# Splitting the small tables one pass per step over the first two tiles, and evicting the counts by plain copies

## Chip, cores, metric

One core of one Trainium2 chip. The metric is the device time of one execution in microseconds (us), the median of several. Most executions agree within 0.3%. Every run quoted here is in the state called fast. A ratio of two kernels is the mean time of one kernel's fast runs over that of the other's in the same rounds on the same chip, so it isn't quite the ratio of the medians that are quoted. The experiments fell on three different chips; on two of them the kernel before takes 7170 us in place of 5298, which is told with the experiments.

## The reference

A recommender network for 16384 rows: 32 word embeddings of 300 numbers and 3 x 20 embeddings of 64 from small tables are averaged, four more rows are looked up singly, and the 748 features go through dense layers of 1024, 512, 256 and 1, to which a sum of one-column tables is added.

```python
tok = word_emb[token_idx].mean(axis=1)          # 50000 x 300, 32 per row
e1 = emb_mh1[mh1_idx].mean(axis=1)              # 1000 x 64, 20 per row; mh2 (5000), mh3 (10000) alike
o1 = emb_oh1[oh1_idx]                           # 100, 50, 20, 1000 rows, one per row
emb = jnp.concatenate([tok, e1, e2, e3, o1, o2, o3, o4], axis=1)
wide = wide_mh1[mh1_idx].sum(axis=(1, 2)) + ...
h = relu(emb @ W1 + b1); h = relu(h @ W2 + b2); h = relu(h @ W3 + b3)
return sigmoid(h @ Wd + bd + wide)
```

## The kernel before

The work runs in 128 tiles of 128 rows. Word rows are gathered from HBM by indirect DMAs that POOL (GpSimd) issues, 32 per tile (128 rows of 300 each), and DVE (VectorE) adds them up, with the sum in PSUM. Buffers hold 6 groups of two gathers. The small tables (138 slices of 128 rows, 65 columns with the wide one) stay in SBUF, the memory on the chip. For them DVE makes one-hot matrices, TensorE (PE) multiplies them to counts, ACT (ScalarE) evicts the counts from PSUM to fp8, and PE multiplies counts by tables. So that bf16 tables are exact enough, each table is split into three bf16 terms: ACT rounds, DVE subtracts what was rounded off, twice. A tile has 11 steps, and all engines go through their instructions in program order.

```python
def convert_tables():                       # PART = 46 slices, CHUNK = 23
    raws = [load_tables(k * PART, tags[k]) for k in range(2)]
    yield
    for part in range(n_h // PART):
        raw = raws[part]
        for a in range(0, PART, CHUNK):
            rows = raw[:, a : a + CHUNK, :]
            for c in range(3):
                at = part * PART + a
                term = terms[:, at : at + CHUNK, c * ROW : (c + 1) * ROW]
                scale = 2.0 if c == 0 else 1.0
                nc.scalar.activation(term, rows, AF.Copy, scale=scale)
                if c < 2:
                    nc.vector.scalar_tensor_tensor(
                        rows, rows, scale, term, op0=ALU.mult, op1=ALU.subtract)
            yield
        ...

def counts(cnt, hot, i):
    pc = ps_c.tile([P, 2, 2, 512], F32, name="pc")           # one PSUM buffer
    ...                                                      # 12 matmuls
    nc.scalar.activation(cnt[...], pc[...], AF.Copy, scale=0.5, saturate=True)

# a step i of tile t (cut)
hot = one_hots(sc, s, i + 1)                                 # DVE
counts(cnt, hot_now, i)                                      # PE, ACT
if t == 0 and i % 3:
    next(tables_on_chip, None)                               # one whole chunk
toks.to(n_groups * (i + 1) / STEPS)                          # gathers (POOL), additions (DVE)
...                                                          # products with the tables, dense layers
```

## Time and profile before

Three runs: 5286.8, 5298.4 and 5295.36 us, median 5295.36. The profiled execution spans 5284.0.

| stretch of the gathers | us | what sets it |
|---|---|---|
| tile 0 | 75.4 | POOL waits for DVE, which works in turn with ACT on the tables |
| tiles 1 to 125 | 40.0 each | 32 gathers of 0.95 us and 0.30 between them |
| from tile 126 to the end | 201 | TensorE, as far as the trace tells: the dense layers of the last tiles (POOL waits here, and PE is busy 36 to 41 us of every 39 to 42) |

In the group lines the columns are: busy time, mean ns of one instruction, then the idle time ahead of them and what ended most of it. In the timelines: start, length, engine, source line, operation, and in brackets how long the engine had been idle and what released it. The lines themselves stand in the prediction.

### The profile page before, as it was taken

Reading aid. Unit: us, or ns where it says so; the run is one execution under the profiler, and the core shown is the slowest. Engines: PE = TensorE matmul, PEld = TensorE weight load, DVE = VectorE, ACT = ScalarE, POOL = GpSimd, SP = SyncE. Lnnn points to the kernel's source line nnn. Section 1 sums busy time; section 2 is a strip of 40 time slices with the busy share of each in tenths; the row PEclk is TensorE's granted clock in tenths of the full one; section 3 lists DMA queues with packets and bytes.
Section 4 is the critical chain, followed back from the end, with each engine's and each line's share of the span. In section 5 each row is a group of like instructions: output and inputs, shape, how many; then the busy total and the mean of one; then the engine's idle time right before and its main releaser. Section 6 shows DMA issues by size and latency. Waiting matters only on the chain.

```text
span 5284.0 us, 104301 instructions
## 1 busy us (share of the span) xinstructions
PE 5073.1 (96%) x41320; PEld 3160.4 (60%) x41320; DVE 3763.4 (71%) x8014; ACT 2528.4 (48%) x2000; POOL 3881.2 (73%) x4103
## 2 busy tenths in 40 slices
PE   3699999999999999999999999999999999999999
PEld 3556565666565666666566556556656556655658
DVE  6777777777777777777777777777777777777753
ACT  5444444444444444444444445445444444444433
POOL 5777777777777777777777777777777777777762
PEclk9799999999999999999999999999999999999999
DMA  6444444444444444444444444444444444444431
GB/s 167 125 124 126 126 126 126 126 125 125 126 126 126 126 124 126 126 125 126 125 125 125 126 126 125 124 125 126 125 126 125 124 126 125 126 126 125 124 103 34
DMA packets 245354, 652.60 MB, mean 124 GB/s; under 512 B 108977, under 2 KB 111988, under 8 KB 244863
## 3 DMA queue, kind: packets, MB, share of 16 engines
q0 software_dynamic: 196608, 629.41, 43.4%
q1 hardware_dynamic: 48255, 16.53, 1.4%
q8 instruction: 323, 5.29, 0.4%
q14 instruction: 168, 1.38, 0.1%
HBM read 645.59 MB, written 0.07 MB: 122 GB/s over the span
## 4 chain that ended last, share of the span: by engine, by line
PE 26%; DMA 26%; issue 17%; DVE 17%; POOL 12%; ACT 1%; SPq 0%; DVEq 0%; POOLq 0%; ACTq 0%
DMA tok_rows<-in_word_emb_dram,it 25%; PE ph L387 14%; POOL tok_rows L223 12%; PE pg L336 8%; DVE own L214 5%; DVE own L212 3%; PE pc L311 3%; DVE slice L293 3%; DVE row L293 1%; DVE x L378 1%; DVE g L342 1%; DVE own L210 1%; PE po L412 1%; DMA raw<-in_mh_dram 0%; ACT cnt L318 0%
## 5 line engine op out<-in xcount | busy, mean ns | idle before, releaser
L223 POOL DMA_INDIRECT tok_rows<-in_word_emb_dram,it x4096 | 3880.3, 947 | 1324.0 <-issue 754.2
L318 ACT ACTIVATE cnt<-pc 128x1656 fp8e3<-128x1656 f32 (+1 forms) x1408 | 2120.6, 1506 | 2020.2 <-PE pc L311 2004.1
L336 PE MATMUL pg<-terms,cnt 128*128 128x195 bf16 x17664 | 1847.6, 254 | 83.1 <-DVE g L342 81.4
L336 PEld LDWEIGHTS <-cnt 128*128 128x128 fp8e3 x17664 | 1599.5, 144 | 229.1 <-issue 74.9
L387 PE MATMUL ph<-x,w_sb 128*128 128x512 f32 (+5 forms) x3264 | 1458.3, 576 | 0.5 <-DVE x L378 0.5
L214 DVE TENSOR_TENSOR own<-own,tok_rows 128x300 f32<-128x300 f32 x1792 | 857.1, 478 | 715.5 <-DMA tok_rows<-in_word_emb_dram,it 684.8
L387 PE MATMUL ph<-h,w_sb 128*128 128x512 f32 (+2 forms) x2720 | 1211.0, 573 | 0.0
L212 DVE TENSOR_TENSOR own<-own,tok_rows 128x300 f32<-128x300 f32 x1920 | 918.5, 478 | 400.3 <-DMA tok_rows<-in_word_emb_dram,it 348.6
L311 PEld LDWEIGHTS <-row 64*128 64x128 bf16 x16384 | 504.5, 95 | 1083.3 <-DVE own L214 255.7
L293 DVE TENSOR_TENSOR row<-own,sc 128x768 bf16<-128x768 bf16 (+1 forms) x1408 | 761.3, 541 | 156.5 <-PE pc L311 81.7
L311 PE MATMUL pc<-slice,row 64*128 64x138 bf16 x16384 | 759.1, 224 | 115.0 <-ACT cnt L318 72.2
L387 PEld LDWEIGHTS ph<-x,w_sb 128*128 128x128 f32 (+1 forms) x3264 | 560.3, 193 | 397.8 <-issue 394.0
L293 DVE TENSOR_TENSOR slice<-own,sc 128x828 bf16<-128x828 bf16 (+1 forms) x1408 | 796.2, 565 | 0.0
L387 PEld LDWEIGHTS ph<-h,w_sb 128*128 128x128 f32 x2720 | 463.1, 192 | 318.4 <-issue 316.3
L396 ACT ACTIVATE h<-ph,b_sb 128x512 f32<-128x512 f32 (+2 forms) x476 | 315.3, 662 | 684.8 <-PE ph L387 673.1
L342 DVE TENSOR_REDUCE g<-pg 128x130 f32<-128x390 f32 (+1 forms) x512 | 258.1, 504 | 108.7 <-PE pg L336 108.3
L378 DVE TENSOR_SCALAR x<-pt,scale 128x512 f32<-128x512 f32 (+4 forms) x204 | 137.2, 713 | 5.3 <-PE pt L377 3.4
L377 PE MATMUL pt<-ident,g 128*128 128x128 f32 (+1 forms) x768 | 103.2, 275 | 2.8 <-DVE x L378 2.3
L210 DVE TENSOR_TENSOR own<-tok_rows 128x300 f32<-128x300 f32 x128 | 61.5, 480 | 47.5 <-DMA tok_rows<-in_word_emb_dram,it 44.6
L377 PEld LDWEIGHTS pt<-ident,g 128*128 128x128 f32 (+1 forms) x768 | 85.5, 140 | 6.4 <-DVE x L378 5.4
L214 DVE TENSOR_TENSOR g<-own,tok_rows 128x300 f32<-128x300 f32 x128 | 60.2, 470 | 25.9 <-DMA tok_rows<-in_word_emb_dram,it 21.1
L412 PE MATMUL po<-h,wd_sb 128*1 128x512 f32 (+2 forms) x136 | 60.9, 566 | 0.3
(34 smaller groups left out, 369.1 us busy)
## 6 DMA issues: line engine op xcount, KB each, us to landing
tok_rows<-in_word_emb_dram,it POOLq DMA_INDIRECT x4096
ix<-in_idx_dram SPq DMA_DIRECT2D x128, 32.0 KB
w_sb<-in_W_dram SPq DMA_DIRECT2D x6, 512.0 KB
it<-in_idx_dram SPq DMA_DIRECT2D x32, 64.0 KB
w_sb<-in_W_dram SPq DMA_DIRECT2D x1, 2048.0 KB
raw<-in_mh_dram SPq DMA_DIRECT2D x1, 975.0 KB
out_dram<-h SPq DMA_DIRECT2D x31, 2.0 KB
raw<-in_mh_dram SPq DMA_DIRECT2D x1, 292.5 KB
```

Of the source, the lines that this page charges most:

```text
L212: nc.vector.tensor_add(tok_sum, tok_sum, a)
L214: nc.vector.tensor_add(to, tok_sum, b)
L223: nc.gpsimd.indirect_dma_start(out=rows[:, r * TOK_D : (r + 1) * TOK_D], out_offset=None, in_=word, in_offset=bass.IndirectOffsetOnAxis(ap ...
L293: nc.vector.tensor_tensor(one[:, 0:rows, :].rearrange("p i (n d) -> p i n d", d=2), iota[:, 0:n].rearrange("p (n d) -> p n d", d=2).unsque ...
L311: nc.tensor.matmul(pc[:, f, k // n, at : at + n_h], hot[0][half, k, :], hot[1][half, k, :], start=True, stop=True,)
L318: nc.scalar.activation(cnt[:, :, b : b + rows, :].rearrange("l f (g k) h -> l f g (k h)", g=2), pc[:, :, :, 0 : n * n_h], AF.Copy, scale=0 ...
L336: nc.tensor.matmul(pg[:, j, :], by_slice[:, :, h], terms[:, h, :], start=(h == h0), stop=(h == h1 - 1))
L342: nc.vector.tensor_reduce(g[:, at : at + n * ROW].rearrange("p (f d) -> p f d", f=n), pg[:, 0:n, :].rearrange("p f (c d) -> p f d c", c=3) ...
L377: nc.tensor.transpose(pt[:kk, s * P : (s + 1) * P], chunk(g, k), ident)
L378: nc.vector.tensor_scalar(x[:kk, k, 0:n], pt[:kk, 0:n], scale[:kk, k : k + 1], None, ALU.mult)
L387: nc.tensor.matmul(ph[:, 0:n], weights[:kk, k, m * P : (m + 1) * P], src[:kk, k, 0:n], start=(k == 0), stop=(k == len(kks) - 1),)
L396: nc.scalar.activation(dst[:, m, 0:n], ph[:, 0:n], AF.Relu, bias=bias[:, m : m + 1])
```

## The change

It intends to keep the first tile from standing still while the tables are split, and to take the clamp out of the count eviction, which a count of at most 20, halved, doesn't need (the results stay correct). A generator now yields after each of 18 passes in place of 6 chunks of five passes, and hands out 1.2 passes per step from step 3 on, so that the last is done in step 17 (step 6 of the second tile), just ahead of the products that need it. DVE's pass needs an ACT pass that is usually a step old. Loads go in parts of 23 slices, and the dense weights are loaded at the end of tile 1.

```diff
-    PART, CHUNK = n_h // 3, n_h // 6
+    PART = n_h // 6
...
         for part in range(n_h // PART):
+            rows = raws[part]
+            if 1 <= part < n_h // PART - 1:
+                raws.append(load_tables((part + 1) * PART, tags[(part + 1) % 2]))
+            for c in range(3):
+                term = [terms[..., k * ROW : (k + 1) * ROW] for k in range(3)]
+                if c:
+                    nc.vector.scalar_tensor_tensor(
+                        rows, rows, 2.0 if c == 1 else 1.0, term[c - 1], op0=ALU.mult, op1=ALU.subtract)
+                nc.scalar.activation(term[c], rows, AF.Copy, scale=2.0 if c == 0 else 1.0)
+                yield 1
...
-            saturate=True,
+            saturate=False,
...
-                if t == 0 and i % 3:
-                    next(tables_on_chip, None)
-                if t == 0 and i == STEPS - 1:
+                tables_on_chip.to(TABLE_PACE * (t * STEPS + i - 2))      # TABLE_PACE = 1.2
+                if t == 1 and i == STEPS - 1:
                     load_weights()
```

More of the change, by code (lines that the diff above doesn't have):

```diff
@@ L30 @@
 CHUNK_WORK = 1
+TABLE_PACE = 1.2
 LAYER_TIME = 10
@@ L165, in convert_tables @@
         for part in range(n_h // PART):
-            raw = raws[part]
-            for a in range(0, PART, CHUNK):
-                rows = raw[:, a : a + CHUNK, :]
-                for c in range(3):
-                    at = part * PART + a
-                    term = terms[:, at : at + CHUNK, c * ROW : (c + 1) * ROW]
-                    scale = 2.0 if c == 0 else 1.0
-                    nc.scalar.activation(term, rows, AF.Copy, scale=scale)
-                    if c < 2:
-                        nc.vector.scalar_tensor_tensor(
-                            rows, rows, scale, term, op0=ALU.mult, op1=ALU.subtract
-                        )
-                yield
-            if part + 2 < n_h // PART:
-                raws.append(load_tables((part + 2) * PART, tags[part % 2]))
+            rows = raws[part]
+            if 1 <= part < n_h // PART - 1:
+                raws.append(load_tables((part + 1) * PART, tags[(part + 1) % 2]))
+            for c in range(3):
+                term = [
+                    terms[:, part * PART : (part + 1) * PART, k * ROW : (k + 1) * ROW]
+                    for k in range(3)
+                ]
+                if c:
+                    nc.vector.scalar_tensor_tensor(
+                        rows, rows, 2.0 if c == 1 else 1.0, term[c - 1], op0=ALU.mult, op1=ALU.subtract
+                    )
+                nc.scalar.activation(term[c], rows, AF.Copy, scale=2.0 if c == 0 else 1.0)
+                yield 1
     w1_sb = const.tile([P, NK, D1], F32, name="w1_sb")
@@ L470 @@
     next(tables_on_chip)
+    tables_on_chip = Paced(tables_on_chip)
     sc = key_columns(lookup_keys(ix))
@@ L516 @@
         before = cnt if t < tiles else None
-        if t == 0:
-            for _ in tables_on_chip:
-                pass
         if len(gs) == sizes[0]:
```

## The prediction

> **What bounds the kernel now.** I read the page first, then the POOL timeline, then the order of work in the first tile, then a table of stretches. The work runs in 128 tiles of 128 rows; each tile gathers 32 token columns, one indirect DMA each, issued by POOL.
>
> ```profile
> PE 5073.1 (96%) x41320; PEld 3160.4 (60%) x41320; DVE 3763.4 (71%) x8014; ACT 2528.4 (48%) x2000; POOL 3881.2 (73%) x4103
> PE   3699999999999999999999999999999999999999
> POOL 5777777777777777777777777777777777777762
> L223 POOL DMA_INDIRECT tok_rows<-in_word_emb_dram,it x4096 | 3880.3, 947 | 1324.0 <-issue 754.2
> ```
>
> PE at 96% looks like the bound. The last line says otherwise: 4096 gathers of 947 ns, with 1324.0 us of idle time ahead of them, which is 0.32 us each, put down to "issue". So POOL does one gather after another, and 4096 x (0.947 + 0.30) is already 5108 us of the 5284. The POOL timeline shows that beat, and where it is lost:
>
> ```profile
> 15.78 0.95 POOL L223 DMA_INDIRECT tok_rows<-in_word_emb_dram,it  x1 [0.30 <-issue]
> 17.03 0.95 POOL L223 DMA_INDIRECT tok_rows<-in_word_emb_dram,it  x1 [0.30 <-issue]
> 33.24 0.95 POOL L223 DMA_INDIRECT tok_rows<-in_word_emb_dram,it  x1 [15.27 <-DVE own L210]
> ...
> 38.24 0.95 POOL L223 DMA_INDIRECT tok_rows<-in_word_emb_dram,it  x1 [0.30 <-issue]
> 39.49 2.46 POOL L223 DMA_INDIRECT tok_rows<-in_word_emb_dram,it  x1 [0.30 <-issue]
> 45.55 0.94 POOL L223 DMA_INDIRECT tok_rows<-in_word_emb_dram,it  x1 [3.60 <-DVE own L214]
> ...
> 75.94 0.95 POOL L223 DMA_INDIRECT tok_rows<-in_word_emb_dram,it  x1 [7.10 <-DVE own L214]
> ```
>
> Starts are 1.25 us apart, so a tile costs 32 x 1.25 = 40.0 us of issuing. The first tile's 32 gathers start at 3.07, and the first gather of the second tile starts at 78.44: 75.4 us, 35.4 us over the beat, in waits for DVE to add up rows and free a buffer. Taking every 32nd gather's start from the trace, each of the tiles 1 to 125 takes 40.0 us (the longest 40.3), and only the last two take 60.2, because their share of the dense layers is larger. So: first tile 75.4, then 125 tiles on POOL's beat, then from 5083 to 5284 a stretch in which PE is truly the bound. Why DVE is late in the first tile:
>
> ```profile
> 16.83 1.47 ACT L173 ACTIVATE terms<-raw 128x1495 bf16<-128x1495 f32 x1 [2.20 <-DMA raw<-in_mh_dram]
> 18.33 1.72 DVE L175 SCALAR_TENSOR_TENSOR raw<-raw,terms 128x1495 f32<-128x1495 f32 x1 [6.71 <-ACT terms L173]
> 20.08 1.47 ACT L173 ACTIVATE terms<-raw 128x1495 bf16<-128x1495 f32 x1 [1.78 <-DVE raw L175]
> 21.58 1.72 DVE L175 SCALAR_TENSOR_TENSOR raw<-raw,terms 128x1495 f32<-128x1495 f32 x1 [1.53 <-ACT terms L173]
> ...
> 24.70 1.52 ACT L318 ACTIVATE cnt<-pc 128x1656 fp8e3<-128x1656 f32 x1
> ```
>
> One piece of table (23 slices of 65) is split into three bf16 terms by ACT and DVE in turn: three ACT passes of 1.47 and two DVE passes of 1.72, each waiting for the other, about 8 us in which neither does anything else. The count eviction, ready since about 15.6, waits until 24.70. Six pieces do this in the first tile. The other matter is ACT's tables:
>
> ```profile
> 554.32 1.28 ACT L420 ACT_TABLE_LOAD   x1
> 556.29 0.68 ACT L420 ACTIVATE h<-po,bd_sb 1x512 f32<-1x512 f32 x1 [0.69 <-PE po L416]
> 556.99 1.28 ACT L318 ACT_TABLE_LOAD   x1
> 558.28 1.55 ACT L318 ACTIVATE cnt<-pc 128x1656 fp8e3<-128x1656 f32 x1
> ```
>
> Each sigmoid costs a load before it and one before the next count eviction. Two stretches, the first without such a pair and the second with it (columns: length, PE, PEld, DVE, ACT, POOL busy and their counts, clock, DMA share, GB/s):
>
> ```profile
> 480.00:520.00 40.00, 39.80 (x319) 24.06 (x318) 27.43 (x59) 18.60 (x15) 30.26 (x32) 1.00 0.45 124
> 520.00:560.00 40.00, 38.85 (x314) 23.45 (x314) 27.57 (x60) 21.78 (x18) 30.26 (x32) 1.00 0.46 125
> ```
>
> ACT is 3.2 us busier in the second and PE is 1 us less busy, but POOL issues 32 gathers in both.
>
> **What the Trainium skill says.** "ScalarE: Activation LUTs", section "What ACT_TABLE_LOAD costs": about 1283 ns for any set, and a drain on top; the trace has the same 1.28 us. The same page, section "Step-by-step: what each stage is for", gives one element per cycle and lane whatever the function, so a plain copy should be no faster than the clamping function; the trace of before has only the clamped form (1548 ns for 1656 elements) and a plain copy from SBUF (1466 ns for 1495), about the same per element. "FP8 and Floating Point Precision", section "Saturation and Rounding": the plain conversion does not saturate; a count beyond the range would matter to values, not to time. "SBUF — State Buffer", section "Who interferes with whom": a DVE instruction with two SBUF inputs contends with a GpSimd instruction that reads SBUF, and the second blocks. The trace agrees: the gather at 39.49 lasted 2.46 us instead of 0.95 beside the DVE pass from 39.42 to 41.14 (both inputs in SBUF), and two more, at 49.31 and 61.09, lasted 1.92 and 1.96.
>
> **The change part by part.**
> 1. Table loads. In the built programs ACT has 64 table loads before and 2 after: the clamped copy is a function of a set that has no sigmoid, the plain copy is in sigmoid's set. That removes 62 x 1.283 = 79.5 us of ACT busy time. I expect none of it on the path: POOL keeps its beat across the loads, and in the PE-bound end only the two pairs at 5158 and 5161 and the load at 5221 are left, where PE has other matmuls. Worth 0, at most 2 us.
> 2. Eviction itself: 1408 x the same duration. Worth 0.
> 3. Staggering. The same 18 ACT passes and 12 DVE passes remain, but one pass per step over steps 3 to 17 (11 steps a tile) instead of three per step in seven steps. In the new order a DVE pass needs an ACT pass of an earlier step, except in the steps with two passes (step 3, step 8, step 13). An ideal beat would bring the first tile from 75.4 to 40.0: worth 35.4.
> 4. What is given back. (a) The lock: a gather starts every 1.25 us, so each DVE pass of 1.72 meets at least one; from the three seen the extra is 1.5, 1.0, 1.0, and for a random phase about 1.6 - 0.63 = 1.0 us. 12 x 1.0 = 12 us. (b) DVE itself: a step needs two one-hots (0.54 + 0.57) and some 1.45 row-pair additions (2 x 0.48 each), 2.5 us; 15 steps with 12 passes are 37.5 + 20.6 = 58.1 us, plus about 2 us of waiting in each of the three double steps, 64 us, against 15 x 3.64 = 54.6 of the beat. POOL starts these steps some 4 us ahead in buffers. So DVE holds POOL back by 5 to 6 us. (a) and (b) overlap, since a POOL that waits for a buffer isn't hurt by the lock: I take 12 us together, over the first two tiles.
> 5. Weights are loaded a tile later (5.3 MB around 80 us instead of 42). First used in tile 5, at about 200 us: worth 0. Table loads of 23 slices: in the chain of waits, 46 slices took 11.9 us from 34.17, so 23 take about 6 to 7; they have two to three steps, 7 to 11 us, from buffer free to use: 0 to 2 us, inside the 12.
>
> Sum: 35.4 - 12 = 23 us, so 5295 - 23 = 5272; I say 5271, because two of the three runs before lie near the top of their spread (5286.8 to 5298.4). The profiled span should go from 5284 to about 5261.
>
> **The rivals.** (A) PE or ACT is the bound in the steady state, so that 31 pairs of loads are each worth 2.6 us: 80 us, and with the start 103, giving 5192, just at 2%. For it: PE at 39.8 of 40.0 us. Against it: 125 tiles of exactly 40.0 us, with and without loads, with and without dense layers. (B) The conversion is hidden completely: 5260. The lock speaks against it, seen three times. (C) Splitting is merely moved: the loads of parts 2 to 5 come late, or the queue order of ACT passes before the next count eviction makes two tiles of 52 us each: saving 11, 5284. For it: ACT is in order and counts have one PSUM buffer. Against: ACT needs only 1.55 + 1.47 = 3.0 of 3.64 us a step. (D) The first product of tile 1 with a table part that isn't ready would stall PE; by the order, part k is complete at steps 4, 7, 9, 12, 14, 17 and first used one to seven steps later, and PE has 27 of 40 us of work in tile 1: no loss.
>
> **Range and chances.** The saving lies between 11 (C) and 35 (B), with 23 likeliest; the median of three runs moves by about 5 by itself. 8 in 10: 5258 to 5285. Faster by over 2% needs more than 106 us, which only A nearly gives: 0.01. Slower by over 2%: 0.01. Within: 0.98.
>
> **What would show it.** Right: ACT busy falls by about 80 to some 2450; first gathers of tiles 1 and 2 start near 50 and 95 (78.44 and 118.47 before); gathers of 1.5 to 2.5 us beside DVE passes, a dozen of them; all later tiles 40.0 us; the stretch from tile 126 on still 201 us. Wrong: a tile below 40.0 us in the middle (POOL wasn't the beat), or tiles 0 and 1 at 40 (no lock), or waits of ACT for table data in tile 1.

## The result, and the profile after

The changed kernel took 5272.2 us (four runs, 5271.1 to 5273.52), the kernel before 5295.3 (four runs). The ratio is 0.9959, with an interval of 0.9942 to 0.9976: 0.4% faster, which counts as the same at a margin of 2%. The result is correct.

From the page of the changed kernel, the busy times and the gathers' group:

```profile
PE 5094.7 (97%) x41320; PEld 3164.7 (60%) x41320; DVE 3768.8 (72%) x8014; ACT 2447.1 (46%) x1938; POOL 3897.3 (74%) x4103
L224 POOL DMA_INDIRECT tok_rows<-in_word_emb_dram,it x4096 | 3896.4, 951 | 1293.4 <-issue 755.5
```

ACT has 62 instructions and 81 us less: the table loads. POOL's gathers were idle 31 us less ahead of them (1293.4 for 1324.0), and busy 16 us more (3896.4 for 3880.3). The idle time that went is the first tile's. Part of the busy time that came is seen in the first two tiles, in this timeline of the changed kernel (some lines of other work left out):

```profile
19.53 1.46 ACT L180 ACTIVATE terms<-raw 128x1495 bf16<-128x1495 f32 x1
...
21.03 1.72 DVE L177 SCALAR_TENSOR_TENSOR raw<-raw,terms 128x1495 f32<-128x1495 f32 x1 [4.22 <-ACT terms L180]
22.07 1.50 POOL L224 DMA_INDIRECT tok_rows<-in_word_emb_dram,it  x1 [0.30 <-issue]
22.78 1.47 ACT L180 ACTIVATE terms<-raw 128x1495 bf16<-128x1495 f32 x1 [1.78 <-DVE raw L177]
...
24.15 1.53 ACT L319 ACTIVATE cnt<-pc 128x1656 fp8e3<-128x1656 f32 x1
...
24.72 1.71 DVE L177 SCALAR_TENSOR_TENSOR raw<-raw,terms 128x1495 f32<-128x1495 f32 x1
25.16 2.09 POOL L224 DMA_INDIRECT tok_rows<-in_word_emb_dram,it  x1 [0.30 <-issue]
...
46.49 0.95 POOL L224 DMA_INDIRECT tok_rows<-in_word_emb_dram,it  x1 [0.30 <-issue]
47.74 1.58 POOL L224 DMA_INDIRECT tok_rows<-in_word_emb_dram,it  x1 [0.30 <-issue]
...
94.17 0.94 POOL L224 DMA_INDIRECT tok_rows<-in_word_emb_dram,it  x1 [0.31 <-issue]
```

Three things are to be seen. A count eviction now follows one ACT pass, or two in the three steps that hand out two passes (the step shown is one of them), and no longer three with two DVE passes between. POOL doesn't wait for a buffer until tile 126: the longest gap between two gathers is 0.35. And a gather that starts during a DVE pass is held up until about that pass's end, and then takes its own 0.95: the one at 22.07 lasted 1.50, a hold of 0.55 us, to 22.62, and the pass ends at 22.75. (The prediction and the expectations call this the lock.)

The gather at 47.74 is the first of tile 1, the one at 94.17 the first of tile 2. The first gather of all starts at 3.12. So the two tiles took 44.6 and 46.4 us, 91.1 together, where before they took 75.4 + 40.0 = 115.4. That is 24.4 us gained, and 10.8 over two tiles at the 40.12 that this execution's later tiles take. All twelve DVE passes prolong one gather each, and the excess over 0.947 adds up to 10.6 us.

The profiled spans differ by 14.7 us only (5284.0 and 5269.3), for a reason that has nothing to do with the change: in the profiled execution of before, the tiles 2 to 125 took 40.04 us on average, in that of after 40.12, and 124 x 0.08 = 9.9. Three of the four other runs of before, 5295 to 5298, are some 10 us slower than its profiled one (5285.8); the fourth took 5286.8. This is taken up below.

### The profile page after: what moved, and what is told of

It is laid out like the page before. It is cut to its first block, busy times and chain, and to the rows that moved or that the text cites. A ratio compares the mean times of both kernels' runs of the same rounds, so it can differ in the third digit from the quotient of the medians.

```text
span 5269.3 us, 104252 instructions
## 1 busy us (share of the span) xinstructions
PE 5094.7 (97%) x41320; PEld 3164.7 (60%) x41320; DVE 3768.8 (72%) x8014; ACT 2447.1 (46%) x1938; POOL 3897.3 (74%) x4103
## 4 chain that ended last, share of the span: by engine, by line
PE 37%; DMA 23%; DVE 16%; issue 14%; POOL 10%; ACT 0%; DVEq 0%; SPq 0%; POOLq 0%; ACTq 0%
DMA tok_rows<-in_word_emb_dram,it 22%; PE ph L388 20%; PE pg L337 12%; POOL tok_rows L224 10%; DVE own L215 5%; PE pc L312 4%; DVE own L213 3%; DVE slice L294 3%; DVE row L294 2%; DVE x L379 1%; DVE g L343 1%; PE po L413 1%; DVE own L211 0%; DVE g L215 0%; PE po L417 0%
## 5 line engine op out<-in xcount | busy, mean ns | idle before, releaser
L224 POOL DMA_INDIRECT tok_rows<-in_word_emb_dram,it x4096 | 3896.4, 951 | 1293.4 <-issue 755.5
L319 ACT ACTIVATE cnt<-pc 128x1656 fp8e3<-128x1656 f32 (+1 forms) x1408 | 2121.7, 1507 | 2056.4 <-PE pc L312 2026.0
L388 PE MATMUL ph<-x,w_sb 128*128 128x512 f32 (+5 forms) x3264 | 1474.1, 581 | 4.2 <-DVE x L379 3.5
```

The costliest lines, as they stand in the source:

```text
L224: nc.gpsimd.indirect_dma_start(out=rows[:, r * TOK_D : (r + 1) * TOK_D], out_offset=None, in_=word, in_offset=bass.IndirectOffsetOnAxis(ap ...
L319: nc.scalar.activation(cnt[:, :, b : b + rows, :].rearrange("l f (g k) h -> l f g (k h)", g=2), pc[:, :, :, 0 : n * n_h], AF.Copy, scale=0 ...
L388: nc.tensor.matmul(ph[:, 0:n], weights[:kk, k, m * P : (m + 1) * P], src[:kk, k, 0:n], start=(k == 0), stop=(k == len(kks) - 1),)
```

## The experiments

There were twelve runs. The first four fell on one chip, where the kernel before takes 5298 us. The eight others fell on two chips where the kernel before takes 7169 and 7172, and it is told below what they can and can't say.

### Which part of the change counts

`stagger_only` keeps the clamped eviction; `plain_only` is the kernel before with plain copies alone.

```diff
 # stagger_only, from the changed kernel
-            saturate=False,
+            saturate=True,
 # plain_only, from the kernel before
-            saturate=True,
+            saturate=False,
```

> The change without its second part: staggered splitting, but count evictions by the clamping function, so 64 table loads stay. Start theory (all of the gain is the first tile's gathers, the table loads are hidden): 5272 us, the same as the changed kernel within 3 us, ACT busy some 80 us more than there. Rival (table loads are part of the gain): the loads of 31 blocks would be worth at least 0.2 us each, so 5278 or more.

> The kernel before with only the evictions changed to plain copies: 2 table loads. Start theory: 5295 us, ratio to before 1.000 within 0.001, the first tile's gathers still 75 us. Rival (loads on the path): up to 80 us less, 5215, or at least some 5 us.

Measured: `stagger_only` 5271.35 us against 5298.15 for before, ratio 0.9951 (0.9937 to 0.9964), correct. `plain_only` 5299.65 us, ratio 1.0003 (0.9994 to 1.0011), correct. Busy times of `stagger_only`, then of `plain_only`:

```profile
PE 5071.5 (96%) x41320; PEld 3160.8 (60%) x41320; DVE 3763.9 (72%) x8014; ACT 2527.2 (48%) x2000; POOL 3887.6 (74%) x4103
```

```profile
PE 5084.9 (96%) x41320; PEld 3159.0 (60%) x41320; DVE 3766.7 (71%) x8014; ACT 2445.2 (46%) x1938; POOL 3880.8 (73%) x4103
```

The 82 us of ACT time come and go with the kind of copy (2527.2 with the clamp, 2445.2 without), and the time doesn't. The eviction is no faster as a plain copy either. So the whole gain is the staggering, and the table loads were hidden, as far as an interval of 0.1% can tell. (The smaller loads of table parts and the later load of the weights belong to the staggering here; they weren't tried apart.) The profiled executions of before and `stagger_only` happen to share the same gather interval (1.251 us), so they can be set side by side: 5284.0 - 5259.3 = 24.7 us, of which tiles 0 and 1 account for 115.4 - 91.1 = 24.3.

### What is left in the first two tiles

`no_pass` drops the twelve DVE passes, so the second and third terms aren't residuals; the result is wrong on purpose (relative error 0.075).

```diff
-                if c:
-                    nc.vector.scalar_tensor_tensor(
-                        rows, rows, 2.0 if c == 1 else 1.0, term[c - 1], op0=ALU.mult, op1=ALU.subtract
-                    )
```

> The changed kernel without its 12 DVE passes of 1.72 us (wrong result on purpose: the second and third terms are not residuals). Lock theory: the 11 us that the gathers of tiles 0 and 1 take beyond 2 x 40.1 are all from DVE passes with two SBUF inputs that hold up a gather's start, so the gathers of the two tiles take 80.3 us and the whole 5261. Rival (ACT's order of passes and evictions with one PSUM buffer for counts, or table data that comes late): the two tiles stay near 91 us and the whole near 5272.

Measured: 5261.97 us (ratio to before 0.9932, 0.9919 to 0.9946), 9.4 us under `stagger_only` of the same rounds. The timeline of its POOL, first gathers of tiles 1 and 2:

```profile
43.51 0.95 POOL L220 DMA_INDIRECT tok_rows<-in_word_emb_dram,it  x1 [0.30 <-DVE own L211]
...
83.57 0.95 POOL L220 DMA_INDIRECT tok_rows<-in_word_emb_dram,it  x1 [0.30 <-DVE keys L263]
```

With a first gather at 3.14 the two tiles take 80.4 us, against 91.1 with the passes. ACT's passes, the evictions, the one PSUM buffer and the later loads of table parts are all still there, so none of them costs anything; the rival that named them falls. But this run takes DVE's time away along with whatever the passes hold. The next pair separates the two.

### Is it the two inputs in SBUF?

160 idle passes are put into tiles 20 to 99, as long as those of the splitting, with a result that nothing reads. In `two_sbuf` both inputs lie in SBUF, in `one_sbuf` the second comes from PSUM.

```diff
+                if 20 <= t < 100 and i in (3, 7):
+                    nc.vector.scalar_tensor_tensor(
+                        scratch, w1_sb[...],                # 23 x 65 numbers from SBUF
+                        1.0,
+                        terms[:, 0:23, 0:ROW],              # two_sbuf
+                        # own[:, 0:ROW] broadcast to 23     # one_sbuf: own is in PSUM
+                        op0=ALU.mult, op1=ALU.subtract)
```

> The changed kernel plus two idle DVE passes (1495 elements, both inputs in SBUF, result unused) in each of tiles 20 to 99, where DVE is idle 12 of 40 us: 160 passes of 1.7 us. Lock theory: each holds up a gather by 0.9 us, so these 80 tiles take 41.9 us instead of 40.1 and the whole is 5272 + 144 = 5416. Rival (gathers are slowed only where DVE is late with additions): DVE has the time, so 5272.

> The same 160 idle DVE passes, but with the second input from PSUM, so one input in SBUF. Lock theory: no gather is held up, 5272. Rival (it is DVE's time or its lateness that counts): the same time as with both inputs in SBUF.

Measured, on a chip where the kernel before took 7168.65 us: `two_sbuf` 7141.53 (ratio 0.9963), `one_sbuf` 7196.31 (ratio 1.0039), both correct. Both were sent once more as `two_sbuf_b` and `one_sbuf_b`, and fell on another chip of that kind:

> 160 idle DVE passes with both inputs in SBUF in tiles 20 to 99, again, on a chip in the usual state. On the slow chip POOL's busy time rose by 124 us over the twin with one SBUF input (4004 against 3880), 0.8 us a pass, and the time did not, as POOL was not the bound there. Lock theory: here the same 125 to 150 us show in the time: 5272 + 125 to 150 = 5397 to 5422. Rival (DVE has the time): 5272.

> The twin with the second input from PSUM, again, on a chip in the usual state. Lock theory: 5272. Rival (DVE's time counts): the same as with two SBUF inputs.

7132.59 (0.9946) and 7197.77 (1.0043), with 7172.14 for before. In time, the expectation of the lock theory for a usual chip wasn't put to the test, because here POOL waits in every tile and isn't what sets the pace. What POOL itself does is as good as on any chip. The idle passes of `two_sbuf` and its gathers:

```profile
L503 DVE SCALAR_TENSOR_TENSOR scratch<-w_sb,terms x160: 1705/1708/1711, 1116.7 to 5495.0; 128x1495 bf16<-128x1495 f32 x160
```

```profile
L225 POOL DMA_INDIRECT tok_rows<-in_word_emb_dram,it x4096 | 4004.3, 978 | 3055.8 <-DVE own L216 1521.3
```

and those of `one_sbuf` (the three numbers of a pass are the shortest, median and longest in ns):

```profile
L503 DVE SCALAR_TENSOR_TENSOR scratch<-w_sb,own x160: 1701/1704/1707, 1117.4 to 5545.1; 128x1495 bf16<-128x1495 f32 x160
```

```profile
L225 POOL DMA_INDIRECT tok_rows<-in_word_emb_dram,it x4096 | 3880.1, 947 | 3239.4 <-DVE own L216 1782.3
```

The passes last the same, 1.71 and 1.70 us. The gathers are busy 4004.3 us with two inputs from SBUF and 3880.1 with one, 124.2 us more; the repeats give 4000.7 and 3881.3. Not all of that is the hold. Gather by gather, 119 gathers of `two_sbuf` begin during one of the 160 passes. All of them last 1.37 to 2.43 us, 0.94 us over the usual on average, which is 111.5 us; nearly all the rest is 3 ns on every gather, the kind of difference between executions that was met above. In `one_sbuf` 97 gathers begin during a pass, and none lasts over 0.955. So DVE's time alone holds no gather up.

The twins differ in more than where the second input lies: it is bf16 in the one, f32 and repeated 23 times in the other. The kernel's own additions, which the trace of before shows, settle that. The first addition of a tile takes both rows from SBUF (L210), the next ones take one row from SBUF and the sum from PSUM (L212), with the same operation, types and shape:

```profile
2325.83 0.48 DVE L210 TENSOR_TENSOR own<-tok_rows 128x300 f32<-128x300 f32 x1
2325.90 1.23 POOL L223 DMA_INDIRECT tok_rows<-in_word_emb_dram,it  x1 [0.31 <-DMA tok_rows<-in_word_emb_dram,it]
...
2329.64 0.48 DVE L212 TENSOR_TENSOR own<-own,tok_rows 128x300 f32<-128x300 f32 x1
2329.93 0.94 POOL L223 DMA_INDIRECT tok_rows<-in_word_emb_dram,it  x1 [0.30 <-DVE slice L293]
```

Of the 40 gathers that begin during an addition of the first kind, 18 are prolonged, up to 1.23 us; the other 22 begin within its last 0.12 us or its first 0.02. Of 1260 that begin during one of the second kind (L212 and L214 into `own`), none lasts over 0.96. So in these passes it is the second SBUF input that holds a gather up. One SBUF input alone is no guarantee, though: in the same trace gathers that began during the integer passes of L260 and L261, with one input, from SBUF, took up to 1.06 us. Where POOL has idle time, as on these chips, the hold is absorbed: `two_sbuf` isn't slower than its twin. It is even 0.8% faster, both times (7141.53 for 7196.31, 7132.59 for 7197.77), and the runs don't show why; that stays open.

### Can the hold be made smaller?

`pieces3` cuts each pass into three, right result.

```diff
-                    nc.vector.scalar_tensor_tensor(rows, rows, ..., term[c - 1], ...)
+                    for h in range(0, PART, 8):
+                        piece = rows[:, h : min(h + 8, PART), :]
+                        nc.vector.scalar_tensor_tensor(piece, piece, ..., term[c - 1][:, h : min(h + 8, PART), :], ...)
```

> The changed kernel with each DVE pass cut into three of 8, 8 and 7 slices (0.6 us each), one behind the other; right result. If the lock is taken for each instruction, and a waiting gather gets in between two pieces, it waits for the rest of one piece: about 0.3 us a pass in place of 0.9, so 12 x 0.3 = 4 us over the beat instead of 11, and 5265 us. If back-to-back pieces keep it out, the extra per pass stays at 0.9 and the time at 5272 or a little above.

Measured: 5272.76 us, ratio 0.9953, the same as `stagger_only` in the same rounds (0.9951). A miss in the time, and yet the hold did shrink. Taking every gather of tiles 0 to 2 that lasted over 1.25 us, four are left with 1.8 us of excess in place of twelve with 10.6; with the smaller ones it is 3.3 us. But three waits of POOL came up that the changed kernel doesn't have, 6.7 us together (counting what exceeds the usual gap of 0.30). This is the second of them, in the timeline of `pieces3`, and below it the same place in the changed kernel:

```profile
41.29 1.46 ACT L182 ACTIVATE terms<-raw 128x1495 bf16<-128x1495 f32 x1
...
42.19 0.95 POOL L226 DMA_INDIRECT tok_rows<-in_word_emb_dram,it  x1 [0.30 <-issue]
42.78 1.85 DVE L179 SCALAR_TENSOR_TENSOR raw<-raw,terms 128x520 f32<-128x520 f32 x3 [2.26 <-ACT terms L182]
44.55 0.47 DVE L215 TENSOR_TENSOR own<-own,tok_rows 128x300 f32<-128x300 f32 x1
...
45.06 0.48 DVE L217 TENSOR_TENSOR own<-own,tok_rows 128x300 f32<-128x300 f32 x1
45.57 0.48 DVE L215 TENSOR_TENSOR own<-own,tok_rows 128x300 f32<-128x300 f32 x1
45.81 0.95 POOL L226 DMA_INDIRECT tok_rows<-in_word_emb_dram,it  x1 [2.67 <-DVE own L217]
```

```profile
42.35 1.72 DVE L177 SCALAR_TENSOR_TENSOR raw<-raw,terms 128x1495 f32<-128x1495 f32 x1 [2.27 <-ACT terms L180]
42.91 1.98 POOL L224 DMA_INDIRECT tok_rows<-in_word_emb_dram,it  x1 [0.30 <-issue]
```

It is a step that hands out two passes, so DVE stands 2.26 us until ACT has made the term, with the step's row additions behind it in its queue, and POOL has no free buffer until they are done. In the changed kernel the same wait of DVE is there (2.27 at 42.35), but POOL, held up four times by then, comes to the point later and finds its buffer free. The hold and DVE's lateness are in parallel, and taking away the longer lets the other show. This is read from the two traces; the run that was to test it comes next.

`pieces3_late` also puts the step's additions ahead of the table step:

```diff
-                tables_on_chip.to(TABLE_PACE * (t * STEPS + i - 2))
                 if t == 1 and i == STEPS - 1:
                     load_weights()
                 toks.to(n_groups * (i + 1) / STEPS)
+                tables_on_chip.to(TABLE_PACE * (t * STEPS + i - 2))
```

> The changed kernel with each DVE pass in three pieces, and the table step now after the step's row additions instead of ahead of them (right result). In the run with pieces alone the gathers of tiles 0 to 2 still lost some 10 us: the holding up of gathers fell to 2.5 us, but POOL waited 6.7 us for additions that stood in DVE's queue behind a pass that waited for ACT. If that reading is right, the additions now go first, the waits go, and 3 to 5 us are lost instead of 11: 5265 us, and tiles 0 and 1 together take 83 to 86 us. Rival (the holding up comes back in another place, or count evictions are later now and the waits only move): 5272.

Measured: 7125.52 us, correct, on a chip where the kernel before took 7172.14; ratio 0.9937 (0.9917 to 0.9956). Next to it, `two_sbuf_b` had 0.9946 there (0.9928 to 0.9964), so no gain of this order can be told on that chip. Whether this order beats the changed kernel on a usual chip stays open.

### Is TensorE the bound in the middle?

`pe_light` leaves out half of the second layer's contraction, `gathers30` two of 32 gathers per tile. Both were meant as wrong results; the comparison's tolerance let both pass.

```diff
 # pe_light
-        yield from layer(h2, w2_sb, b2_sb, h1, [P] * M1, M2, n)
+        yield from layer(h2, w2_sb, b2_sb, h1, [P] * (M1 // 2), M2, n)
 # gathers30
-    n_groups = N_TOK // TOK_GROUP
+    n_groups = N_TOK // TOK_GROUP - 1
```

> The changed kernel with half of the second dense layer's contraction left out (wrong result on purpose): some 3.4 us less TensorE work per tile of 40 (16 matmuls of 0.86 us per block of four tiles). Gather theory (POOL's 32 gathers of 1.25 us set each tile): tiles 2 to 125 stay at 40.1 us; only the end, from tile 126 on, gets shorter, by some 25 us: 5247. Rival (TensorE at 97% is the bound): 124 x 3.4 = 420 us less, 4850.

> The changed kernel with 30 of 32 token gathers per tile (wrong result on purpose). Gather theory: the beat of a tile falls from 40.1 to 30 x 1.253 = 37.6 us unless TensorE, next in line with 39.x busy, holds it: I expect TensorE to take over at 38.5 to 39.5 us a tile, so 5080 to 5210 us, with POOL now waiting for DVE. Rival (TensorE is the bound already): unchanged, 5272.

> The run with 30 of 32 gathers again, as the first fell on a chip on which every kernel, the one before too, takes 7170 us and POOL waits in every tile. On a chip with 5295 us for the kernel before: gather theory: TensorE takes over at 38.5 to 39.5 us a tile, 5080 to 5210 us. Rival (TensorE is the bound already): 5272.

Measured: `pe_light` 6990.14 us (ratio 0.9762), `gathers30` 6801.23 (0.9491), `gathers30_b` 6797.19 (0.9481), on the chips with 7169 and 7172 us for before. None of the expectations for a usual chip could be read off these. What such a chip does is seen in `one_sbuf`, in a part of the first tile where its program is that of the changed kernel:

```profile
11.05 1.55 ACT L320 ACTIVATE cnt<-pc 128x1656 fp8e3<-128x1656 f32 x1 [9.03 <-PE pc L313]
12.66 0.87 PE L313 MATMUL pc<-slice,row 64*128 64x138 bf16 x12 [2.23 <-ACT cnt L320]
...
18.82 1.55 ACT L320 ACTIVATE cnt<-pc 128x1656 fp8e3<-128x1656 f32 x1 [6.21 <-remote]
```

PE's twelve matmuls are recorded as done at 13.53, but ACT, which waits for them, starts at 18.82. On the usual chip the same eviction starts within 0.1 us of the matmuls. Such gaps recur through the whole run: of the 1172 evictions in it that ACT stood ready for, 458 began more than 1 us after the last of their matmuls, some by 9 us and more, and of 1009 in the profile of before not one. The mean granted clock is 0.88 to 0.92 on these chips, against 0.99 on the usual one. DVE, ACT and POOL instructions last as long as elsewhere (gathers 947 ns). What makes those gaps is not shown. On these chips POOL waits for DVE 1724 us in all in `pe_light`, so it isn't the bound there, and less of either work shortens the run. For the usual chip the question was not answered by an experiment; the evidence there is the traces alone (next section).

## Why the prediction was right

The prediction said 5271 us and a profiled span of 5261, and 5272.2 was measured. The profiled span of after was 5269.3; the one of `stagger_only`, which ran at the gather interval of before's profile, was 5259.3.

1. *The gathers are the beat.* Shown as far as traces go: in all six profiled executions on usual chips POOL doesn't wait between tile 2 and tile 125 (no gap is over 0.32 us but one of 0.77 and one of 0.59, at the very end of tile 125), a tile takes 40.0 to 40.1 us on average, and a change of the interval shows in full: `pieces3` was profiled at 1.254 us and `stagger_only` at 1.251, so 4096 x 0.003 = 12 us are expected between them and 5270.7 - 5259.3 = 11.4 are there. What happens at the start reaches the end unchanged: the stretch from tile 126 on took 200.8 to 201.1 us in all six. That a lighter TensorE would leave the middle as it is was argued and not shown.
2. *Table loads worth 0.* Shown by `plain_only` and `stagger_only`.
3. *The eviction costs the same.* Right: its group's mean is 1506 ns with the clamp and 1507 without.
4. *Staggering worth 35.4, less 12.* 24.3 to 24.4 of 35.4 were measured in the first two tiles, so 11 given back. The tiles began at 47.74 and 94.17, where the prediction had near 50 and 95.
5. *The two costs behind the 12.* Term (a), the hold of one gather per DVE pass, was sized at 1.0 us each and is 10.6 / 12 = 0.88; it is the whole of the loss. Term (b), DVE 5 to 6 us late, doesn't appear in the changed kernel: POOL waits for no buffer before tile 126. A wait of about its size, 6.7 us, comes out in `pieces3`, as soon as the hold is cut. The reason given for the overlap, that a POOL waiting for a buffer isn't hurt by the hold, is the wrong way round: the hold slowed POOL so far that it waited for no buffer. By the prediction's own figures, an estimate, 11 us of holds stretch the 15 steps from 54.6 to some 65 us, and DVE needs 64. The overlap was assumed and not worked out, and that the sum came out right is partly luck.
6. *Weights and parts in time.* Right: the changed kernel's list of waits has none for table data, and `no_pass`, with the same loads, runs its two tiles in 80.4 us.

## What to carry to other kernels

A unit at 97% busy need not be the one that sets the pace: count what each queue takes at the least per round, and look for the one that never waits. If the pace is set by an engine that issues one thing after another, work moved elsewhere gains only where that engine stands still; here that was at the start, and it arrived in full. And before cutting a cost that lies beside another, ask how late the other would be without it: here cutting the hold to a third brought nothing, and the traces show why: a wait of nearly the same size had been lying under it.

## What the Trainium skill lacked or had wrong

- "SBUF — State Buffer", section "Who interferes with whom": its list of what grabs the shared pair says, as inferred, that `tensor_tensor` doesn't stall descriptor generation because it takes only the read interface. A two-input DVE pass, and a plain `tensor_tensor` addition of two SBUF rows too, does hold up an indirect gather's issue: each of the 119 gathers that began during a pass with two SBUF inputs, by 0.94 us on average, and none of 97 with the second input in PSUM; 18 of 40 that began during such an addition. The rule further up in that section, about a GpSimd instruction that reads SBUF, fits. That an indirect gather is such an instruction isn't said.
- "DMA: Bandwidth & Descriptors": I found no figure for what one indirect gather costs its issuing engine. Here 128 rows of 1200 bytes take POOL 0.947 us and 0.30 to the next, unless DVE holds it up as above.
- No page that I read has the two gather intervals, 1.251 and 1.254 us, between which executions of one program differ (12 us of 5290). In four of the six kernels on usual chips the profiled execution was 9.5 to 14 us faster than the others' median.
- "ScalarE: Activation LUTs", section "What ACT_TABLE_LOAD costs", adds a drain of about 1380 ns to a switch. In the trace of before the load takes 1.28 us, starts 0.02 us after the instruction ahead of it (556.97 to 556.99) and the next eviction starts as it ends (558.27 to 558.28); it is 0.01 to 0.02 us on either side of all 31 loads between a sigmoid and an eviction. So no drain is seen on ACT.
- No page that I read told me to expect chips on which the same program takes 7170 us in place of 5295, with gaps of 1 to 9 us after matmuls and a mean granted clock of 0.88 to 0.92.
